# A graph-attention layer on one core: where the last eight blocks of x are loaded and added

## The chip, the core and the metric

The kernel runs on one core of a Trainium2 chip. The core has a matrix engine (TensorE, PE in the profile), a vector engine (VectorE, DVE), an activation engine (ScalarE, ACT), a general engine (GpSimd, POOL) and a sequencer that mostly issues transfers (SyncE, SP). Each takes its instructions in order; they wait for one another by semaphores. The metric is the device time of one execution in microseconds, as the median of several runs.

## What is computed

```python
ht = (h @ W).reshape(N, 4, 512)            # 4 heads
e = leaky_relu(src[:, :, None] + dst[:, None, :], 0.01) + adj[None]
att = softmax(e, axis=-1)
x_out = layernorm(x + mean_over_heads(att @ ht))
```

Here x is 4096 x 512 and adj is 4096 x 4096, both float32; W is 512 x 2048. The entries of adj go up to 1e9 and lie far apart, so that a row's softmax is 1 at the row's largest entry and 0 elsewhere as long as the largest entry leads the second by more than a bound on the other terms. Then a row of the output is layernorm(x[i] + x[j] @ mean of the heads' W), with j the column of the largest entry of row i of adj.

## The kernel before, in words

The rows are dealt out to 128 partitions in 32 blocks (NB = 32): partition p has rows 32 p to 32 p + 31, and block ib is row 32 p + ib of every partition. A block of adj is 2 MB, a block of x, of gathered rows or of the output 256 KB. `LATE` is 28, `Q` is 4.

`leading_rows` does the work above for all rows, and counts the rows in which the largest entry does not lead by enough. `general` (a full softmax for such rows) runs only if there are any; with these inputs it does not run.

The main loop runs over t = 0 to 31, and each pass works on several blocks:

- SyncE issues the load of adj block t + 5 (`load_adj`, six buffers), and in some passes a load of x into `hold` (`load_x`). All loads go through one queue in the order of issue, so a block of adj that stands behind a block of x lands after it. A block of adj comes in 1, 2 or 4 pieces (`pieces`).
- VectorE takes the maximum of each 64 entries of block t (`segment_maxima`, line 155; in two groups, with `find_column` of block t - 2 between them) and finds the segment with the row's maximum (`find_segment`).
- GpSimd fetches that segment's 64 entries (`lead`, line 168). Two passes later VectorE finds the column in it (`find_column`, line 190) and, for the later test, the two largest of it (`find_inner`, line 184). GpSimd then gathers the row of x that belongs to the column (`y`, line 178).
- TensorE transposes y of block t - 3 (`turn`, line 205), ScalarE copies the result out (line 207), TensorE puts x of the block into PSUM by a product with the identity (`residual`, line 211) and adds y times the mean W in four products (`products`, line 218; each is two matmul records in the trace).
- ScalarE sums block t - 4 and its squares (`stats`, lines 230 and 232) and the squares of x (`row_norm`, line 225), GpSimd makes the reciprocal deviation of two blocks (`rstd`, lines 235 to 237), and ScalarE normalises blocks t - 6 and t - 5 (`finish`, line 241).

After the loop comes the drain, written out by hand. For the last block `find_column_in_row` scans the whole row of adj (line 198), which needs no fetched segment. The last four blocks are normalised by `finish_last` on VectorE: add x (line 247), mean and variance (250, 252), a square root on ScalarE (254), reciprocal (255), scale (256). `bound`, `test`, `count` and `report` make the count of rows that don't lead; `bound` needs the row norms of all of x, `test` all of `inner`. SyncE issues the stores of the output (`store`, line 259) behind all loads: six of 1 MB for blocks 0 to 23, one of 256 KB for each later block; ScalarE issues block 31's.

The order around the change is thus set by three things: SyncE's queue, the order of the instructions on each engine as the code writes them, and the buffers. Before the change, `x_at` puts x of blocks 24 to 27 between the adj loads (x of 24 is ahead of adj 27, and so on), and x of 28 to 31 comes as one load of 1 MB behind all of adj.

Of the kernel before, what the change touches and what calls it, by code (L numbers as in the profile page):

```python
# [9 lines left out]
F32 = mybir.dt.float32  # L10
# [9 lines left out]
P = 128  # L20
C = 512
E = 64
# [43 lines left out]
def leading_rows(ctx, tc, x, adj, W, a, out, ident, v, n_bad, any_bad):  # L66
# [4 lines left out]

    nc = tc.nc
    N, D = x.shape
    H = a.shape[0]
    KB, NB, S = D // P, N // P, N // E
    AHEAD = 5
    Q = 4
    PIECES = 4  # L80
    LATE = NB - Q

    once = ctx.enter_context(tc.tile_pool(name="once", bufs=1))
    adj_pool = ctx.enter_context(tc.tile_pool(name="adj_pool", bufs=AHEAD + 1))
# [15 lines left out]
    adj_t = {}  # L100

    def pieces(ib):
        return PIECES if ib in (0, LATE, NB - 1) else 2 if ib > LATE else 1

    def load_adj(ib):
        if 0 <= ib < NB:
# [5 lines left out]
    def load_x(lo, n):  # L112
        nc.sync.dma_start(hold[:, ds(lo, n), :], x_rows[:, ds(lo, n), :])
# [46 lines left out]
    def find_segment(ib):  # L160
        seg = seg_of.pop(ib)
        nc.vector.max(out=top[:, ib, :], in_=seg)
        at = small.tile([P, 8], U32, name="at")
        nc.vector.max_index(at, top[:, ib, :], seg)  # L164
        row = small.tile([P, 1], U32, name="row")
        nc.gpsimd.tensor_tensor(row, at[:, 0:1], first[:, ib : ib + 1], op=OP.add)  # L166
        lead = small.tile([P, E], F32, name="lead")
        nc.gpsimd.indirect_dma_start(  # L168
            out=lead, out_offset=None, in_=adj_segs,
            in_offset=bass.IndirectOffsetOnAxis(ap=row[:, :1], axis=0),  # L170
        )
        start = at_of[ib] = small.tile([P, 1], U32, name="start")
        nc.gpsimd.tensor_tensor(start, at[:, 0:1], width, op=OP.mult)  # L173
        lead_of[ib] = lead
# [8 lines left out]
    def find_inner(ib):  # L183
        nc.vector.max(out=inner[:, ib, :], in_=lead_of[ib])

    def find_column(ib):
        if ib != NB - 2:
            find_inner(ib)
        within = small.tile([P, 8], U32, name="within")
        nc.vector.max_index(within, top[:, ib, :], lead_of[ib])  # L190
        col = small.tile([P, 1], U32, name="col")
        nc.gpsimd.tensor_tensor(col, at_of.pop(ib), within[:, 0:1], op=OP.add)  # L192
        gather_rows(ib, col)
# [7 lines left out]
    def turn(ib):  # L201
        y = y_t.pop(ib)
        tp = psum.tile([P, KB, P], F32, name="tp", bufs=2)
        for kb in range(KB):
            nc.tensor.transpose(tp[:, kb, :], y[:, ts(kb, P)], ident)  # L205
        yt = yt_of[ib] = rows.tile([P, KB, P], F32, name="yt")
        nc.scalar.copy(yt, tp)  # L207
# [5 lines left out]
    def products(ib, lo=0, hi=KB):  # L213
        start = ib not in o_ps
        if start:
            o_ps[ib] = psum.tile([P, D], F32, name="o")
        for kb in range(lo, hi):
            nc.tensor.matmul(  # L218
                o_ps[ib], yt_of[ib][:, kb, :], w_sum[:, kb, :],
                start=(start and kb == 0), stop=(kb == KB - 1),  # L220
            )

    def row_norm(ib):
        sq = rows.tile([P, D], F32, name="sq")
        nc.scalar.activation(sq, hold[:, ib, :], AF.Square, accum_out=xx[:, ib : ib + 1])  # L225

    def stats(ib):
        o, i = o_ps[ib], slice(ib, ib + 1)
# [5 lines left out]
    def rstd(i):  # L234
        nc.gpsimd.tensor_scalar(sd[:, i], sd[:, i], 1.0 / D, EPS, op0=OP.mult, op1=OP.add)  # L235
        nc.gpsimd.tensor_tensor(sd[:, i], sd[:, i], power[:, : i.stop - i.start], op=OP.pow)  # L236
        nc.gpsimd.tensor_mul(nm[:, i], nm[:, i], sd[:, i])  # L237

    def finish(ib):
        i = slice(ib, ib + 1)  # L240
        nc.scalar.activation(hold[:, ib, :], o_ps.pop(ib), AF.Identity, bias=nm[:, i], scale=sd[:, i])  # L241

    def finish_last(ib, residual):

        o = o_ps.pop(ib)
        if residual:
            nc.vector.tensor_add(hold[:, ib, :], o, hold[:, ib, :])
            o = hold[:, ib, :]
        st = small.tile([P, nc.vector.BN_STATS_DIM], F32, name="st", bufs=2)
        nc.vector.bn_stats(st, o)  # L250
        mv = small.tile([P, nc.vector.BN_AGGR_DIM], F32, name="mv", bufs=2)
        nc.vector.bn_aggr(mv, st)
        r = small.tile([P, 1], F32, name="r", bufs=2)
        nc.scalar.activation(r, mv[:, 1:2], AF.Sqrt, bias=eps)
        nc.vector.reciprocal(r, r)
        nc.vector.tensor_scalar(hold[:, ib, :], o, mv[:, 0:1], r, op0=OP.subtract, op1=OP.mult)

    def store(queue, lo, n):
        queue.dma_start(out_rows[:, ds(lo, n), :], hold[:, ds(lo, n), :])
# [49 lines left out]
    def bound(part):  # L309

        if part == 0:
            xm = once.tile([P, 1], F32, name="xm")
            nc.vector.tensor_reduce(xm, xx, axis=AX.X, op=OP.max)
            px = of_bound[0] = psum.tile([1, P], F32, name="px", bufs=1)
            nc.tensor.transpose(px, xm, ident)
        elif part == 1:
            nc.vector.tensor_reduce(xg, of_bound[0], axis=AX.X, op=OP.max)
            nc.scalar.activation(xg, xg, AF.Sqrt)
            pb = of_bound[1] = psum.tile([P, 1], F32, name="px", bufs=1)
            nc.tensor.matmul(pb, ones[0:1, :], xg, start=True, stop=True)  # L320
        else:
            nc.vector.tensor_mul(lead_by, of_bound[1], vn)
            nc.vector.tensor_scalar(lead_by, lead_by, 1.05, 110.0, op0=OP.mult, op1=OP.add)
# [18 lines left out]
    def report(pg):  # L342
        nc.vector.tensor_scalar(n_bad, pg, -1.0, float(P), op0=OP.mult, op1=OP.add)
        total = once.tile([1, 1], F32, name="total")
        nc.vector.tensor_reduce(total, pg, axis=AX.X, op=OP.add)
        nc.vector.tensor_scalar(any_bad, total, -1.0, float(N), op0=OP.mult, op1=OP.add)

    x_at = {lo - 1: (lo, Q) for lo in range(Q, LATE - Q, Q)}
    x_at.update({ib - 2: (ib, 1) for ib in range(LATE - Q, LATE)})
    vectors = [(kb, h) for kb in range(KB) for h in range(H)]  # L350
    vectors_at = {t: 2 if t < 3 else 1 for t in range(1, 15)}
    COLUMN, PROJECT, STATS, FINISH = 2, 3, 4, 6
# [1 line left out]
    for t in range(NB):  # L354
        if t in x_at:
            load_x(*x_at[t])
        load_adj(t + AHEAD)
        middle = 1 if t == NB - 1 else 2
        segment_maxima(t, 0, middle)
        if t >= COLUMN:  # L360
            find_column(t - COLUMN)
        segment_maxima(t, middle, PIECES)
        pair = t >= FINISH and t % 2 == 0
        if pair:
            rstd(slice(t - FINISH, t - FINISH + 2))
        find_segment(t)
        if t < 2:
            mean_of_heads(t)
        elif t == 2:
            mean_of_heads(2)  # L370
            mean_of_heads(3)
        if t == 0:
            turn_a()
        turned = [(*vectors[0], turn_w(*vectors.pop(0))) for _ in range(vectors_at.get(t, 0))]
        if t == 16:
            head_norms()
        ib = t - PROJECT
        if ib >= 0:
            turn(ib)
            if ib < LATE:  # L380
                residual(ib)
        for some in turned:
            head_vector(*some)
        if ib >= 0:
            products(ib)
        if t >= STATS:
            stats(t - STATS)
            row_norm(t - STATS)
        if pair:
            finish(t - FINISH)  # L390
            finish(t - FINISH + 1)

    load_x(LATE, NB - LATE)
    for lo in range(0, NB - 2 * Q, Q):
        store(nc.sync, lo, Q)
    for ib in range(NB - 2 * Q, NB - FINISH):
        store(nc.sync, ib, 1)
    find_column(NB - 2)
    rstd(slice(NB - FINISH, NB - FINISH + 2))
    find_column_in_row(NB - 1)  # L400
    for ib in range(LATE, NB):
        row_norm(ib)
    turn(NB - 3)
    products(NB - 3, 0, KB - 1)
    finish(NB - FINISH)
    finish(NB - FINISH + 1)
    bound(0)
    finish_last(NB - 4, True)
    find_inner(NB - 2)
    find_inner(NB - 1)  # L410
    turn(NB - 2)
    products(NB - 3, KB - 1, KB)
    residual(NB - 1)
    products(NB - 2, 0, 1)
    bound(1)
    products(NB - 2, 1, KB - 1)
    finish_last(NB - 3, True)
    turn(NB - 1)
    bound(2)
    test()  # L420
    products(NB - 2, KB - 1, KB)
    for ib in range(NB - FINISH, NB - 2):
        store(nc.sync, ib, 1)
    products(NB - 1, 0, KB - 1)
    pg = count()
    products(NB - 1, KB - 1, KB)
    finish_last(NB - 2, True)
    store(nc.sync, NB - 2, 1)
    report(pg)
    finish_last(NB - 1, False)  # L430
    store(nc.scalar, NB - 1, 1)

# [233 lines left out]
```

## Time and profile before

| what | us |
|---|---|
| median of 7 runs | 247.32 (246.19 to 248.61) |
| the profiled execution's own time | 246.12 |
| its span in the profile | 244.1 |
| PE busy | 197.0 (81%) |
| DVE busy | 186.1 (76%), of which line 155: 146.1 |
| ACT busy | 109.8 (45%) |
| POOL busy | 97.4 (40%) |
| bytes moved by DMA | 97.76 MB, mean 401 GB/s |

The profile is of one execution. All times in it count from the start of its span. A line of the timeline has the start, the duration, the engine, the line of the kernel, the operation, output<-input with shapes, and in brackets how long the engine was idle before it and what ended that wait. A line of the chain of work has start, duration and what ran. A line of the table by stage has the stage, its length, the busy time of PE, PE's weight loads, DVE, ACT and POOL with the number of instructions, the granted clock of TensorE, the busy share of the DMA engines and what they moved in GB/s.

### The profile page before, as it was taken

What the parts mean: (1) busy time and instruction counts of PE and PEld (TensorE: products, weight loads), DVE (VectorE), ACT (ScalarE), POOL (GpSimd) and SP (SyncE); (2) the same over time, 40 slices, a digit from 0 to 9 for tenths busy, and PEclk for the clock granted to TensorE, in tenths of its full rate; (3) what the DMA queues carried; (4) which work ended last, traced back from release to release, by engine and by line L of the source; (5) the groups of instructions that cost most, each with busy time, mean ns of one, the idle gap of its engine ahead of it and who ended that gap; (6) DMA issues with size and microseconds to landing.
All of it is one profiled execution on the core that took longest, in us unless ns stands there. A gap on an engine that the chain in (4) does not pass through costs nothing.

```text
span 244.1 us, 2481 instructions
## 1 busy us (share of the span) xinstructions
PE 197.0 (81%) x677; PEld 99.3 (41%) x678; DVE 186.1 (76%) x300; ACT 109.8 (45%) x266; POOL 97.4 (40%) x213
## 2 busy tenths in 40 slices
PE   0269749999999899999959977798768989877970
PEld 0125326556565556655324423343323433332520
DVE  2645685399689886999589969985998998978561
ACT  2012002145757574757635653556344846476110
POOL 1202422226525643645254636453546464653000
PEclk9999989999999999999988999999999999999995
DMA  7999999999999999999999999999999999999971
GB/s 258 434 430 412 418 430 419 413 424 424 408 419 417 405 431 417 415 408 433 412 421 414 424 411 418 414 416 420 423 416 389 407 407 406 404 426 424 419 281 55
DMA packets 13988, 97.76 MB, mean 401 GB/s; under 512 B 2184, under 2 KB 2184, under 8 KB 7824
## 3 DMA queue, kind: packets, MB, share of 16 engines
q1 hardware_dynamic: 10224, 87.82, 87.2%
q0 software_dynamic: 3584, 9.44, 9.9%
q10 hardware_dynamic: 160, 0.28, 0.3%
q8 instruction: 7, 0.11, 0.2%
q14 instruction: 13, 0.11, 0.1%
HBM read 89.15 MB, written 8.39 MB: 400 GB/s over the span
## 4 chain that ended last, share of the span: by engine, by line
issue 37%; POOL 34%; DMA 18%; PE 4%; DVE 3%; POOLq 1%; SPq 1%; ACT 0%
DMA adj_t<-in_adj_dram 15%; POOL lead L168 11%; POOL y L178 11%; POOL sd L236 4%; PE o L218 3%; DMA y<-in_x_dram,col 3%; POOL start L173 2%; POOL col L192 2%; POOL row L166 2%; DVE seg L155 2%; POOL sd L235 1%; POOL nm L237 1%; SPq L110 1%; POOLq L178 0%; PE tp L205 0%
## 5 line engine op out<-in xcount | busy, mean ns | idle before, releaser
L155 DVE TENSOR_REDUCE seg<-adj_t 128x32 f32<-128x2048 f32 (+1 forms) x70 | 146.1, 2093 | 40.5 <-DMA adj_t<-in_adj_dram 40.0
L218 PE MATMUL o<-w_sum,yt 128*128 128x512 f32 x256 | 119.8, 609 | 1.5 <-ACT yt L207 1.5
L218 PEld LDWEIGHTS o<-w_sum,yt 128*128 128x128 f32 x256 | 46.5, 192 | 58.4 <-issue 45.4
L207 ACT COPY yt<-tp 128x512 f32<-128x512 f32 x32 | 18.8, 587 | 49.0 <-PE tp L205 42.7
L178 POOL DMA_INDIRECT y<-in_x_dram,col x32 | 30.8, 964 | 17.8 <-POOL col L192 15.7
L168 POOL DMA_INDIRECT lead<-in_adj_dram,row x32 | 32.2, 1008 | 13.9 <-POOL row L166 13.9
L205 PE MATMUL tp<-ident,y 128*128 128x128 f32 x128 | 19.7, 277 | 16.6 <-DMA y<-in_x_dram,col 16.5
L264 PE MATMUL o<-hold,ident 128*128 128x512 f32 x32 | 17.9, 713 | 17.9 <-DMA hold<-in_L_gnn_W_dram 17.9
L211 PE MATMUL o<-hold,ident 128*128 128x512 f32 x58 | 29.9, 598 | 0.0
L192 POOL TENSOR_TENSOR col<-start,within 128x1 uint32<-128x1 uint32 x31 | 5.9, 189 | 52.5 <-DVE within L190 52.5
L205 PEld LDWEIGHTS tp<-ident,y 128*128 128x128 f32 x128 | 14.1, 141 | 31.1 <-issue 27.6
L282 ACT COPY wt<-tp 128x512 f32<-128x512 f32 x16 | 9.2, 587 | 31.6 <-PE tp L280 30.0
L166 POOL TENSOR_TENSOR row<-at,first 128x1 uint32<-128x1 uint32 x32 | 6.1, 189 | 37.8 <-DVE at L164 37.8
L241 ACT ACTIVATE hold<-o,nm,sd 128x512 f32<-128x512 f32 x28 | 20.1, 770 | 0.0
L225 ACT ACTIVATE sq<-hold 128x512 f32<-128x512 f32 x32 | 19.8, 618 | 0.0
L232 ACT ACTIVATE sq<-o,nm 128x512 f32<-128x512 f32 x28 | 19.3, 688 | 0.9
L288 PEld LDWEIGHTS pv<-at_d,wt 128*128 128x128 f32 x128 | 16.3, 191 | 6.8 <-ACT wt L282 3.5
L264 PEld LDWEIGHTS o<-hold,ident 128*128 128x128 f32 x32 | 7.0, 229 | 26.2 <-POOL row L166 10.4
L265 ACT ACTIVATE w_sum<-o 128x512 f32<-128x512 f32 x4 | 2.4, 598 | 33.5 <-PE o L264 33.5
L230 ACT ACTIVATE sq<-o 128x512 f32<-128x512 f32 x28 | 17.0, 606 | 0.0
L288 PE MATMUL pv<-at_d,wt 128*128 128x2 f32 x128 | 15.3, 244 | 0.6 <-ACT wt L282 0.6
L280 PEld LDWEIGHTS tp<-ident,hold 128*128 128x128 f32 x64 | 7.9, 142 | 6.9 <-issue 6.9
(73 smaller groups left out, 115.7 us busy)
## 6 DMA issues: line engine op xcount, KB each, us to landing
adj_t<-in_adj_dram SPq DMA_DIRECT2D x27, 2048.0 KB, 33.5
hold<-in_x_dram SPq DMA_DIRECT2D x7, 1024.0 KB, 34.0
adj_t<-in_adj_dram SPq DMA_DIRECT2D x12, 512.0 KB, 10.3
out_dram<-hold SPq DMA_DIRECT2D x6, 1024.0 KB, 21.8
hold<-in_L_gnn_W_dram SPq DMA_DIRECT2D x4, 1024.0 KB
adj_t<-in_adj_dram SPq DMA_DIRECT2D x4, 1024.0 KB
out_dram<-hold SPq DMA_DIRECT2D x7, 256.0 KB, 3.0
hold<-in_x_dram SPq DMA_DIRECT2D x4, 256.0 KB, 13.1
```

Source lines behind the costliest of these rows:

```text
L155: nc.vector.tensor_reduce(seg_of[ib][:, ts(k, S // n)], adj_t[ib][:, ts(k, N // n)].rearrange("p (s e) -> p s e", e=E), axis=AX.X, op=OP.max,)
L168: nc.gpsimd.indirect_dma_start(out=lead, out_offset=None, in_=adj_segs, in_offset=bass.IndirectOffsetOnAxis(ap=row[:, :1], axis=0),)
L178: nc.gpsimd.indirect_dma_start(out=y, out_offset=None, in_=x, in_offset=bass.IndirectOffsetOnAxis(ap=col[:, :1], axis=0),)
L205: nc.tensor.transpose(tp[:, kb, :], y[:, ts(kb, P)], ident)
L207: nc.scalar.copy(yt, tp)
L211: nc.tensor.matmul(o_ps[ib], ident, hold[:, ib, :], start=True, stop=False)
L218: nc.tensor.matmul(o_ps[ib], yt_of[ib][:, kb, :], w_sum[:, kb, :], start=(start and kb == 0), stop=(kb == KB - 1),)
L225: nc.scalar.activation(sq, hold[:, ib, :], AF.Square, accum_out=xx[:, ib : ib + 1])
L232: nc.scalar.activation(sq, o, AF.Square, bias=nm[:, i], accum_out=sd[:, i])
L241: nc.scalar.activation(hold[:, ib, :], o_ps.pop(ib), AF.Identity, bias=nm[:, i], scale=sd[:, i])
L264: nc.tensor.matmul(o, ident, hold[:, w_at + kb * H + h, :], start=(h == 0), stop=(h == H - 1))
L288: nc.tensor.matmul(pv[:, kb, h : 2 * H : H], wt[:, k, :], at_d[:, k, h : 2 * H : H], start=(k == 0), stop=(k == KB - 1),)
```

## The change

`BEHIND` is 24. x of blocks 24 to 31 is loaded behind all of adj, in eight loads of 256 KB; blocks 24 to 27 have no `residual` in TensorE's sum. In the loop, ScalarE copies the bare products of these four blocks into a buffer of the adj pool (`put_by`) instead of doing `stats`, `row_norm` and `finish` on them. In the drain VectorE adds x to them (`add_x`, both operands in SBUF), ScalarE does their `stats`, GpSimd their `rstd`, and ScalarE normalises them (`finish`). All eight `row_norm`s of blocks 24 to 31 and all eight `find_inner`s stand in the drain. adj blocks 28 to 31 come in four pieces each, and in passes 29 to 31 `find_column` stands behind the first piece instead of behind the first half. All stores have 256 KB, and the last seven are issued by SyncE behind `report`.

```diff
-        return PIECES if ib in (0, LATE, NB - 1) else 2 if ib > LATE else 1
+        return PIECES if ib == 0 or ib >= LATE else 1
...
-        lead = small.tile([P, E], F32, name="lead")
+        lead = small.tile([P, E], F32, name="lead", bufs=2 * Q + 1)
...
-        if ib != NB - 2:
+        if ib < BEHIND:
             find_inner(ib)
...
+    def put_by(ib):
+        if ib == BEHIND:
+            o_ps["by"] = adj_pool.tile([P, N // D, D], F32, name="adj_t")
+        nc.scalar.copy(o_ps["by"][:, ib - BEHIND, :], o_ps.pop(ib))
+
+    def add_x(ib):
+        nc.vector.tensor_add(hold[:, ib, :], hold[:, ib, :], o_ps["by"][:, ib - BEHIND, :])
+        o_ps[ib] = hold[:, ib, :]
...
-    x_at = {lo - 1: (lo, Q) for lo in range(Q, LATE - Q, Q)}
-    x_at.update({ib - 2: (ib, 1) for ib in range(LATE - Q, LATE)})
+    x_at = {lo - 1: (lo, Q) for lo in range(Q, BEHIND, Q)}
...
-        middle = 1 if t == NB - 1 else 2
+        middle = 1 if t > LATE else 2
...
-        pair = t >= FINISH and t % 2 == 0
+        pair = FINISH <= t < BEHIND + FINISH and t % 2 == 0
...
-            if ib < LATE:
+            if ib < BEHIND:
                 residual(ib)
...
-        if t >= STATS:
+        if t >= BEHIND + STATS:
+            put_by(t - STATS)
+        elif t >= STATS:
             stats(t - STATS)
             row_norm(t - STATS)
...
-    load_x(LATE, NB - LATE)
-    for lo in range(0, NB - 2 * Q, Q):
-        store(nc.sync, lo, Q)
-    for ib in range(NB - 2 * Q, NB - FINISH):
+    for ib in range(BEHIND, NB):
+        load_x(ib, 1)
+    for ib in range(BEHIND):
         store(nc.sync, ib, 1)
     find_column(NB - 2)
-    rstd(slice(NB - FINISH, NB - FINISH + 2))
     find_column_in_row(NB - 1)
-    for ib in range(LATE, NB):
+    for ib in range(BEHIND, NB - 2):
         row_norm(ib)
     turn(NB - 3)
+    for ib in range(NB - 2, NB):
+        row_norm(ib)
     products(NB - 3, 0, KB - 1)
-    finish(NB - FINISH)
-    finish(NB - FINISH + 1)
+    finish_last(NB - 4, True)
     bound(0)
-    finish_last(NB - 4, True)
-    find_inner(NB - 2)
-    find_inner(NB - 1)
     turn(NB - 2)
+    add_x(BEHIND)
+    add_x(BEHIND + 1)
     products(NB - 3, KB - 1, KB)
     residual(NB - 1)
     products(NB - 2, 0, 1)
     bound(1)
     products(NB - 2, 1, KB - 1)
+    add_x(BEHIND + 2)
+    add_x(BEHIND + 3)
+    stats(BEHIND)
+    stats(BEHIND + 1)
+    rstd(slice(BEHIND, BEHIND + 2))
     finish_last(NB - 3, True)
+    stats(BEHIND + 2)
     turn(NB - 1)
+    finish(BEHIND)
+    finish(BEHIND + 1)
+    stats(BEHIND + 3)
+    rstd(slice(BEHIND + 2, LATE))
+    for ib in range(BEHIND, NB):
+        find_inner(ib)
     bound(2)
     test()
     products(NB - 2, KB - 1, KB)
-    for ib in range(NB - FINISH, NB - 2):
-        store(nc.sync, ib, 1)
     products(NB - 1, 0, KB - 1)
     pg = count()
     products(NB - 1, KB - 1, KB)
     finish_last(NB - 2, True)
-    store(nc.sync, NB - 2, 1)
+    finish(BEHIND + 2)
+    finish(BEHIND + 3)
     report(pg)
+    for ib in (NB - 4, NB - 3, BEHIND, BEHIND + 1, NB - 2, BEHIND + 2, BEHIND + 3):
+        store(nc.sync, ib, 1)
     finish_last(NB - 1, False)
     store(nc.scalar, NB - 1, 1)
```

More of the change, by code (lines that the diff above doesn't have):

```diff
@@ L81, in leading_rows @@
     LATE = NB - Q
+    BEHIND = LATE - Q
     once = ctx.enter_context(tc.tile_pool(name="once", bufs=1))
```

## The prediction

> **What bounds the kernel now.** I read the page's slices first, then the waits, then the end of the chain of work, then VectorE's timeline over the last blocks, then the table by stage of the DMA rate. The page's span and DMA rows:
>
> ```profile
> span 244.1 us, 2481 instructions
> DMA  7999999999999999999999999999999999999971
> GB/s 258 434 430 412 418 430 419 413 424 424 408 419 417 405 431 417 415 408 433 412 421 414 424 411 418 414 416 420 423 416 389 407 407 406 404 426 424 419 281 55
> ```
>
> The DMA engines are full from 6 us to about 235 us. Only the last 9 us are not transfer. So the order of transfers decides when the last work can begin, and the sum of bytes sets a floor. The chain's end shows what follows the last gathers:
>
> ```profile
> 218.63 7.10 DMA y<-in_x_dram,col
> ...
> 225.86 0.63 PE tp L205 x4
> ...
> 231.72 3.57 PE o L218 x8
> ...
> 238.01 0.81 DVE hold L256
> ```
>
> Block 30's gather lands at 225.72; TensorE then works almost without a gap to 236.5, VectorE normalises block 31 to 238.82, the last store is issued at 238.86. What made that gather start at 218.63 stands in VectorE's timeline:
>
> ```profile
> 187.90 2.29 DVE L155 TENSOR_REDUCE seg<-adj_t 128x32 f32<-128x2048 f32 x1 [0.86 <-DMA adj_t<-in_adj_dram]
> ...
> 190.11 0.22 DVE L184 MAX8 inner<-lead 128x8 f32<-128x64 f32 x1
> 190.24 0.07 DVE L190 MATCH_VALUE_LOAD within<-top,lead 128x8 f32 x1
> ...
> 205.17 2.29 DVE L155 TENSOR_REDUCE seg<-adj_t 128x32 f32<-128x2048 f32 x1 [0.97 <-DMA adj_t<-in_adj_dram]
> ...
> 216.04 0.22 DVE L164 FIND_INDEX8 at<-top,seg 128x8 uint32<-128x64 f32 x1
> 217.48 0.09 DVE L190 MATCH_VALUE_LOAD within<-top,lead 128x8 f32 x1 [1.22 <-DMA lead<-in_adj_dram,row]
> ...
> 217.82 4.42 DVE L198 FIND_INDEX8 col<-top,adj_t 128x8 uint32<-128x4096 f32 x1
> ```
>
> VectorE waits for adj before blocks 27 (0.86) and 30 (0.97); otherwise it is back to back from 187.90 to 216.26, 5.4 to 5.5 us a block. So two limits lie close together: transfers (a 2 MB adj block, a 256 KB x block and a 256 KB gather) and VectorE.
>
> **The change, part by part.**
>
> *x of 24 to 27 leaves the adj stream.* Four x blocks are 1.05 MB; at the 404 to 406 GB/s of that stretch (rows below) 2.6 us. Adj 27 lands 0.65 sooner (one x block was ahead of it), adj 30 and 31 2.6 sooner. VectorE can't take all of it: block 27 starts 0.65 sooner (187.25), block 30's wait of 0.97 goes, and next it is bound by itself.
>
> *find_inner of 24 to 31 moves to the drain.* MAX8 takes the pipe 0.13 (190.11 to 190.24); five blocks on this path save 0.65. Blocks 29 and 30 are reduced in 4 pieces, not 2: 2.33 a half instead of 2.28, about 0.2 back. Sum: block 31's segment search ends 0.65 + 0.97 + 0.65 - 0.1 = 2.2 us sooner, at 214.05 instead of 216.26.
>
> *The column search one piece sooner (29, 30).* The search for block t-2 then stands 5.35 + 1.15 = 6.5 behind that block's own segment search. The lead row it reads took 0.87 to be issued and 5.6 to 6.1 to land: 6.5 to 7.0. At 6.5 nothing waits; at 7.0 VectorE stalls 0.5 in up to three blocks. Beside 4 KB rows the leads landed in the shorter of these times; I take 0.2 in all, bounds 0 and 1.5.
>
> *Last columns.* Lead 30 is issued at about 209.4 and lands by 215.0; block 31's scan of 4.42 runs 215.3 to 219.8 (before 217.82 to 222.24). The gather of y30 keeps its distance of 2.37 from the segment search of 31 (GpSimd does row, lead and start in between): 216.5, and lands 6.1 to 7.1 later (6.1 is a gather beside 4 KB rows in this trace, 7.1 beside 8 KB), 222.6 to 223.6 against 225.72.
>
> *ScalarE in the loop.* A put_by copy (L207's 0.59) replaces stats and row_norm (0.61 + 0.20 + 0.69 + 0.19 + 0.62 + 0.19, less overlap: 2.0). Four residual matmul pairs of 0.86 go too. Neither engine ends a wait there: nothing gained. The eight row_norms (0.61 each, 4.9) stand partly before the copy of yt29. x29 should land near 216, the six norms end near 217 and y29's transposes near 217.8: covered by 0.8, and if x is later the copy is late by as much.
>
> *The drain on VectorE,* from the end of the scan to the last tensor_scalar. Before: 222.24 to 238.82, 16.6, of which 1.98 + 1.27 + 0.60 were waits for TensorE. Added: 4 add_x and 6 more MAX8. add_x reads two SBUF tiles, which no row shows; the nearest is L247 (one PSUM operand) at 0.69. Back to back I take 0.60 to 0.70: 2.4 to 2.8. MAX8: 6 x 0.14 = 0.8. Together 3.2 to 3.6, into waits of 3.85. The waits don't all survive: TensorE's chain also starts sooner. Following the three orders op by op, scan end 219.7, y30 222.6: finish_last(28) to 222.3, two adds and xg to 223.9, two adds to 225.1, finish_last(29) to 228.1 with 0.5 waiting for ScalarE (two stats of 1.41 are queued ahead of its sqrt), MAX8s to 229.3, test to 230.7, finish_last(30) to 233.4, report to 233.8, finish_last(31) to 236.3. ScalarE's last sqrt sits behind finish(26) and finish(27), which wait for stats(27) and a 1.27 us GpSimd chain: 0.2 to 0.3, included. TensorE ends at 233.3 and is not late. With y30 at 223.6 the end is 237.0. So the last store is issued at 236.3 to 237.1, against 238.86.
>
> A rule of the Trainium skill speaks against this part. GPSIMD Engine Reference, section Specifications, says that GpSimd shares its SBUF interface with VectorE and is held up by VectorE instructions with two SBUF inputs. The adds run 222.4 to 225.1, while GpSimd writes y31's descriptors. In the trace y31, issued at 223.00 beside adds with one SBUF operand, was there without a wait when TensorE turned it at 231.12. In the changed kernel it is issued at about 220.5 and lands, at y30's 6.5 or so, at 227. By the rule it could be 2.4 later, 229.4, and TensorE, which wants it at 228.1, would lose 1.3. I take nothing and keep 1.3 as the bound.
>
> *Transfers at the end.* Stores of blocks 0 to 23 become 24 of 256 KB (2 KB rows) instead of six of 1 MB; x 24 to 31 eight loads of 256 KB; blocks 29 and 30 finer. By stage (DMA share and GB/s are the last two columns):
>
> ```profile
> 206.00:212.00 6.00, 4.81 (x15) 1.97 (x14) 5.82 (x11) 2.38 (x7) 3.00 (x8) 1.00 1.02 399
> 212.00:230.00 18.00, 15.00 (x45) 6.81 (x44) 13.73 (x27) 10.82 (x28) 6.56 (x13) 1.00 1.02 424
> 232.00:234.00 2.00, 2.00 (x6) 0.83 (x5) 1.35 (x2) 0.40 (x1) 0.00 (x0) 1.00 1.01 393
> 234.00:236.00 2.00, 2.00 (x8) 0.61 (x6) 1.35 (x7) 0.29 (x1) 0.00 (x0) 1.00 0.70 269
> ```
>
> 206 to 212 is block 31 in quarters, 212 to 230 mostly 1 MB stores, 232 to 234 256 KB stores alone. From 186 to the end the rows add up to 20.9 MB. At 398 GB/s (the finer rows) that takes 52.5 us: to 238.5, where the last bytes before left at about 240.8. The rule of DMA: Bandwidth & Descriptors, section Bandwidth, is to batch DMAs to 1 MiB for 75% of peak, and it puts 1 MB at 341 GB/s and 64 KB at 138. By it, 256 KB stores at some 250 GB/s (an estimate between these figures) would need 33 us for 8.1 MB instead of 20, and the kernel would be 10 us slower. The row decides: several stores are in flight at once, and 256 KB ones ran at 393. Their issues cost SyncE 0.33 each against 0.65 of transfer: hidden.
>
> Compute frees the last store at 236.3 to 237.1; its 1.9 us after that (238.86 to 240.8 before) would end at 238.2 to 239.0; transfers allow 238.5. I take 239.0, which is 1.8 sooner. Span 242.3; that run's own 246.12 becomes 244.3; it stood 1.2 below the median, and the same 1.8 off the median 247.32 gives 245.5.
>
> **Rivals.** (1) *The drain eats it.* VectorE has no slack left after the scan, so each unforeseen wait there (leads 1.0, y31 1.3, ScalarE's order) shows in full. For it: two in-order engines tie at the end. Against: the path's every other duration is in a row. A loss of 1 us more leaves 0.8: 246.5, within 0.5%. (2) *The change does not bring columns sooner*, because VectorE, not adj, is the limit: only the 0.65 and part of 0.97 remain, also about 246.5. Against it: the row at 205.17 waits for DMA. (3) *Slower: the cut stores.* If x and stores of 2 KB rows run below the rest, transfers set the end. It decides once the mean from 186 on falls below 20.9 MB / 54.8 us = 381 GB/s. At 340 for these 10.2 MB and 398 for the other 10.7: 26.9 + 30.0, so 242.9, 2.1 later than before: 249.4. For it: 393 is the lowest full row, and only eight transfers can be outstanding, now 2 MB instead of 8. Against: that row had at most six outstanding.
>
> **How the numbers follow.** About 0.5% (1.2 us) is what a measurement of this kernel can tell from no change. Forecast 0.64 (244.3 to 246.0), rivals 1 and 2 together 0.22 (246 to 247.7), rival 3 0.14 (247.7 to 250). Low end: transfers at 411 GB/s as before end at 236.9 and compute allows 2.6 to 3: 244.3. High end 247.7: leaves out rival 3 and the edge below. Faster 0.64, same 0.22, slower 0.14.
>
> **What would show it.** Right: no DMA wait before block 30's reduce; scan of block 31 starting near 215.3; VectorE almost gapless after it; last store issued near 236.5; 390 to 405 GB/s from 216 to 234. Wrong: the wait for leads in three blocks; a late copy of yt29 or yt31 behind ScalarE's norms or stats; DMA rows under 380 with the last stores queued behind others.

## The result, and the profile after

The changed kernel takes 245.38 us (median of 23 runs, 244.79 to 246.72), the kernel before 246.85 (60 runs, 245.57 to 249.32). The ratio is 0.994 with an interval of 0.9925 to 0.9955: 1.5 us sooner, where 1.8 were forecast. In the experiments each ratio is against runs of the kernel before from the same set (their medians run from 246.51 to 247.16), so it is not exactly the quotient of two medians shown here.

The profiled execution of the changed kernel took 245.75 us. Its span, transfers and rates:

```profile
span 243.7 us, 2537 instructions
...
DMA  6999999999999999999999999999999999999993
GB/s 247 409 426 419 426 422 414 429 415 409 423 416 418 407 427 416 424 406 426 411 419 418 425 420 416 409 420 412 419 422 392 403 403 399 389 393 397 403 376 118
```

The engines that move data are now full to the last slice but one; before, the last two slices read 7 and 1. VectorE's timeline of this execution, at the places that were shown of before:

```profile
182.16 2.29 DVE L157 TENSOR_REDUCE seg<-adj_t 128x32 f32<-128x2048 f32 x1 [0.34 <-DMA adj_t<-in_adj_dram]
...
214.43 0.22 DVE L166 FIND_INDEX8 at<-top,seg 128x8 uint32<-128x64 f32 x1
216.27 0.09 DVE L192 MATCH_VALUE_LOAD within<-top,lead 128x8 f32 x1 [1.63 <-DMA lead<-in_adj_dram,row]
...
216.61 4.42 DVE L200 FIND_INDEX8 col<-top,adj_t 128x8 uint32<-128x4096 f32 x1
```

The wait for adj ahead of block 30 (0.97) is gone, and block 31's segment search comes at 214.43 instead of 216.04. Then VectorE waits 1.63 for the fetched segment of block 30 (1.22 before), so its scan starts only 1.2 sooner.

The chain that ended last, in the same execution (start, duration, what ran):

```profile
215.37 5.40 PE o L220 x8
...
225.30 0.59 ACT yt L209
...
235.37 0.87 ACT hold L253 x2
236.24 0.55 issue
236.79 0.29 ACT r L266
...
237.30 0.81 DVE hold L268
```

Two things are new. The eight product records of block 28 took 5.40; in a second profiled execution of this kernel (below) they took 3.71. And from 225.30 on the chain runs through ScalarE, not through TensorE. The table by stage shows both (the last three columns are the granted clock of TensorE, the share of the transfer engines and GB/s):

```profile
212.00:230.00 18.00, 15.49 (x43) 6.87 (x42) 14.44 (x27) 11.35 (x34) 4.99 (x9) 0.91 1.05 396
...
232.00:234.00 2.00, 2.00 (x7) 0.62 (x5) 1.57 (x4) 1.97 (x6) 0.00 (x0) 1.00 1.05 402
234.00:236.00 2.00, 1.23 (x5) 0.33 (x4) 1.67 (x7) 0.82 (x3) 1.08 (x3) 1.00 0.99 380
```

The granted clock was 0.91 over 212 to 230 (1.00 before) and 0.76 over 214 to 221, and ScalarE is busy nearly all of 232 to 234 (1.97 of 2.00). Since a clock like that may belong to one execution, the same kernel was profiled again, as one of the experiments.

### The profile page after: what moved, and what is told of

It is laid out like the page before. It is cut to its first block, busy times and chain, and to the rows that moved or that the text cites. A ratio compares the mean times of both kernels' runs of the same rounds, so it can differ in the third digit from the quotient of the medians.

```text
span 243.7 us, 2537 instructions
## 1 busy us (share of the span) xinstructions
PE 199.6 (82%) x669; PEld 101.1 (41%) x670; DVE 188.2 (77%) x308; ACT 111.9 (46%) x270; POOL 97.3 (40%) x213
## 4 chain that ended last, share of the span: by engine, by line
issue 34%; POOL 32%; DMA 19%; ACT 4%; PE 4%; DVE 3%; POOLq 1%; SPq 1%; ACTq 0%
DMA adj_t<-in_adj_dram 15%; POOL lead L170 10%; POOL y L180 10%; POOL sd L248 4%; PE o L220 3%; DMA y<-in_x_dram,col 3%; POOL start L175 2%; POOL col L194 2%; POOL row L168 2%; DVE seg L157 2%; ACT sq L244 1%; POOL sd L247 1%; ACT sq L242 1%; POOL nm L249 1%; ACT yt L209 1%
## 5 line engine op out<-in xcount | busy, mean ns | idle before, releaser
L220 PE MATMUL o<-w_sum,yt 128*128 128x512 f32 x256 | 121.3, 615 | 4.2 <-ACT yt L209 4.2
L220 PEld LDWEIGHTS o<-w_sum,yt 128*128 128x128 f32 x256 | 47.4, 195 | 61.1 <-issue 47.3
L207 PEld LDWEIGHTS tp<-ident,y 128*128 128x128 f32 x128 | 14.9, 144 | 25.8 <-issue 25.1
L276 PEld LDWEIGHTS o<-hold,ident 128*128 128x128 f32 x32 | 8.0, 264 | 25.8 <-POOL row L168 11.3
L253 ACT ACTIVATE hold<-o,nm,sd 128x512 f32<-128x512 f32 x24 | 17.2, 771 | 0.0
L244 ACT ACTIVATE sq<-o,nm 128x512 f32<-128x512 f32 x24 | 16.5, 687 | 0.8
L242 ACT ACTIVATE sq<-o 128x512 f32<-128x512 f32 x24 | 14.6, 607 | 0.0
```

The costliest lines, as they stand in the source:

```text
L220: nc.tensor.matmul(o_ps[ib], yt_of[ib][:, kb, :], w_sum[:, kb, :], start=(start and kb == 0), stop=(kb == KB - 1),)
L244: nc.scalar.activation(sq, o, AF.Square, bias=nm[:, i], accum_out=sd[:, i])
L276: nc.tensor.matmul(o, ident, hold[:, w_at + kb * H + h, :], start=(h == 0), stop=(h == H - 1))
```

## The experiments

**The changed kernel once more** (no edit).

> The changed kernel itself, on the same chip as the three beside it: 0.9925 to 0.9955. Theory of the stall (2 KB rows slow the gather of the lead of block 30): its stall before block 31's scan is 1.2 to 1.8 us again, and the scan starts 1.0 to 1.4 us sooner than in the kernel before. Rival (the stall belonged to the one execution, as did TensorE's clock of 0.76): the stall is under 0.7.

245.37 us, ratio 0.9949 (0.9924 to 0.9974). Its profiled execution took 244.77, with a span of 242.8. VectorE's timeline:

```profile
181.43 2.29 DVE L157 TENSOR_REDUCE seg<-adj_t 128x32 f32<-128x2048 f32 x1 [0.35 <-DMA adj_t<-in_adj_dram]
...
213.70 0.22 DVE L166 FIND_INDEX8 at<-top,seg 128x8 uint32<-128x64 f32 x1
215.60 0.09 DVE L192 MATCH_VALUE_LOAD within<-top,lead 128x8 f32 x1 [1.68 <-DMA lead<-in_adj_dram,row]
...
215.93 4.42 DVE L200 FIND_INDEX8 col<-top,adj_t 128x8 uint32<-128x4096 f32 x1
```

The first row stood at 182.16 in the other execution, so that one lagged by 0.7 already there, and keeps that distance to the scan. The stall of 1.7 for the lead is there again. The scan starts 1.9 sooner than before the change, somewhat more than the 1.0 to 1.4 that was expected. The table by stage of this execution:

```profile
212.00:230.00 18.00, 14.60 (x47) 6.87 (x47) 14.95 (x37) 12.84 (x37) 4.56 (x9) 1.00 1.05 398
...
234.00:236.00 2.00, 0.00 (x0) 0.00 (x0) 1.01 (x4) 1.69 (x3) 0.00 (x0) 1.00 1.04 399
236.00:238.00 2.00, 0.00 (x0) 0.00 (x0) 0.74 (x1) 0.00 (x0) 0.00 (x0) 0.81 0.91 344
238.00:239.00 1.00, 0.00 (x0) 0.00 (x0) 0.00 (x0) 0.00 (x0) 0.00 (x0) 0.50 0.74 270
```

The clock is 1.00 here, and the last store is issued at 236.77 (238.14 in the other execution, 238.86 before the change). But the transfer engines are full to 236, busy for 0.91 of the time to 238, and SyncE's last bytes leave at 239.2. So compute and transfers end nearly together here. (In the first execution compute came last: the engines ran at 0.89 from 236 to 238, and the last store was issued 1.4 later.) The next experiments take the two apart.

**Does x, moved behind adj, bring the gain?** x of 24 to 27 back between the adj loads, everything else as changed:

```diff
+    x_at.update({ib - 2: (ib, 1) for ib in range(BEHIND, LATE)})
-    for ib in range(BEHIND, NB):
+    for ib in range(LATE, NB):
         load_x(ib, 1)
```

> Undoes one part of the change: x of blocks 24 to 27 is loaded between the adj blocks again, all else is as in the changed kernel. My theory (the gain comes from adj landing up to 2.6 us sooner, and VectorE takes about 2 of it): the DMA wait before block 30's reduce is back, the scan of block 31 starts 1 to 2 us later than in the changed kernel, and the time goes to 0.998 to 1.004 of the kernel before. Rival (the gain comes from finding the columns one piece sooner and from the lighter loop on ScalarE and TensorE): the time stays at 0.994.

246.54 us, ratio 0.9963 (0.993 to 0.9996). Its timeline of VectorE:

```profile
207.05 2.49 DVE L157 TENSOR_REDUCE seg<-adj_t 128x16 f32<-128x1024 f32 x2 [0.72 <-DMA adj_t<-in_adj_dram]
...
215.95 0.22 DVE L166 FIND_INDEX8 at<-top,seg 128x8 uint32<-128x64 f32 x1
216.40 0.09 DVE L192 MATCH_VALUE_LOAD within<-top,lead 128x8 f32 x1 [0.23 <-DMA lead<-in_adj_dram,row]
```

The waits for adj are back, and block 31's search comes 2.25 later than in the second execution above, which this one matches up to block 26 (181.44 against 181.43). The stall for the lead shrinks from 1.68 to 0.23 at the same time, so the scan (216.73) is only 0.8 later. In the same set of runs the two variants below that keep x behind adj take 245.30 and 245.62. The move is thus worth about 1 us of the 1.5: nine of the twelve runs here (245.67 to 247.09) lie above the slowest of the twelve of x in pairs (244.66 to 245.95), though the intervals of the two ratios overlap. The ratio is lower than the 0.998 to 1.004 that was expected, so part of the gain doesn't hang on the move; which other part of the change brings it, no run here takes apart.

**Are finer last blocks enough?** The kernel before, with only the four pieces for blocks 28 to 31 and the earlier column search:

```diff
-        return PIECES if ib in (0, LATE, NB - 1) else 2 if ib > LATE else 1
+        return PIECES if ib == 0 or ib >= LATE else 1
...
-        middle = 1 if t == NB - 1 else 2
+        middle = 1 if t > LATE else 2
```

> The kernel before with one part of the change alone: adj blocks 28 to 31 in four pieces and the column search behind the first piece in passes 29 to 31. My theory: y of 27 to 29 is gathered 1 us sooner but the scan of block 31 starts at the same time, so 0.999 to 1.001. Rival (late columns carry the gain): 0.996 or below.

247.22 us, ratio 1.0007 (0.9973 to 1.004), scan at 217.87 (217.82 before). These two parts alone bring nothing sooner.

**Do the 2 KB rows of x make the stall?** x of 24 to 31 in four loads of two blocks (4 KB rows):

```diff
-    for ib in range(BEHIND, NB):
-        load_x(ib, 1)
+    for ib in range(BEHIND, NB, 2):
+        load_x(ib, 2)
```

> The changed kernel with x of 24 to 31 in four loads of two blocks (4 KB rows) instead of eight of one (2 KB rows). In the changed kernel's profile the gathers beside 2 KB rows moved their bytes in 2.5 to 3.1 us, beside 4 KB rows in 1.5, and the fetched segment of block 30 came 1.6 us after VectorE was ready. If the row size is the cause: VectorE's wait before block 30's column falls from 1.6 to 0.8 or less, and the kernel gains 0.3 to 1.0 us on the changed one (0.990 to 0.993 of before). If the number of outstanding bytes or something else is the cause: the wait stays at 1.6 and the time at 0.994.

245.30 us, ratio 0.9921 (0.9887 to 0.9955). VectorE's timeline:

```profile
211.05 0.09 DVE L192 MATCH_VALUE_LOAD within<-top,lead 128x8 f32 x1 [0.51 <-DMA lead<-in_adj_dram,row]
...
215.60 0.09 DVE L192 MATCH_VALUE_LOAD within<-top,lead 128x8 f32 x1 [0.22 <-DMA lead<-in_adj_dram,row]
```

The stall for lead 30 falls to 0.22, but 0.51 of it moves to lead 29, and the time stays. So far it looks as if the 2 KB rows made the stall. The other runs' profiles don't bear that out. Eight profiled executions do the same work up to the scan (the two of the changed kernel, and the variants below and after this one that edit only the drain or the stores). In four of them the last bytes of lead 30 came 5.47 to 5.53 after its issue, and the stall was 1.58 to 1.76; in three they came after 4.67 to 4.74, and it was 0.85 to 0.93; in one lead 29 was the late one. Beside 4 KB rows both times are seen too: the two later variants with x in pairs have 4.55 and 4.67 (stalls of 0.80 and 0.90), while here lead 29 took 5.43, and in the kernel before lead 29 took 5.45. So in kernels that are alike up to this point there are two landing times, 0.8 apart (in the kernel before, lead 30 took 5.03, between the two), and a floor of 0.8 to 0.9 under the stall; that 2 KB rows make the later one likelier is not shown. The late lead does not come alone. In the four executions with a late lead 30, the gather y28, still under way when that lead was issued, was late too: its last bytes came 6.9 to 7.2 after its issue, against 5.5 to 5.6 in the three with an early lead; in the one with a late lead 29 it was y27 (7.0, against 5.7). Something holds up GpSimd's gathers once, for about 1 us, and what it is stays open.

**Is it ScalarE's order at the end?** Roots of 26 and 27 apart, and `finish(26)` ahead of block 30's square root:

```diff
     stats(BEHIND + 2)
+    rstd(slice(BEHIND + 2, BEHIND + 3))
     turn(NB - 1)
...
     stats(BEHIND + 3)
-    rstd(slice(BEHIND + 2, LATE))
+    rstd(slice(BEHIND + 3, LATE))
+    finish(BEHIND + 2)
...
-    finish(BEHIND + 2)
     finish(BEHIND + 3)
```

> The changed kernel with GpSimd's reciprocal deviation of blocks 26 and 27 made one by one, and block 26 normalised ahead of block 30's square root. If ScalarE's queue holds the end (its last square root waited 0.6 us behind two normalisations): VectorE's last wait falls from 0.9 to 0.4 us and the kernel gains 0.3 to 0.6 us on the changed one (0.992). If the last stores' transfers hold the end: the wait falls and the time stays at 0.994.

245.62 us, ratio 0.9944 (0.9913 to 0.9975). VectorE's wait ahead of the last reciprocal fell from 0.92 (first execution) to 0.36, the round trip to ScalarE and back; the one ahead of block 30's grew from 0.58 to 1.27:

```profile
235.44 0.17 DVE L267 RECIPROCAL r<-r 128x1 f32<-128x1 f32 x1 [1.27 <-ACT r L266]
...
237.73 0.16 DVE L267 RECIPROCAL r<-r 128x1 f32<-128x1 f32 x1 [0.36 <-ACT r L266]
```

The wait was moved, not removed.

**Do the cut stores hold up the end?** Stores of 0 to 23 in twelve pairs, and, in a second kernel, in six of 1 MB (the same lines with `Q` in place of 2):

```diff
-    for ib in range(BEHIND):
-        store(nc.sync, ib, 1)
+    for ib in range(0, BEHIND, 2):
+        store(nc.sync, ib, 2)
```

> The changed kernel with the stores of blocks 0 to 23 as twelve of two blocks (4 KB rows) instead of twenty-four of one. Theory (the end is set by compute: the last store is issued when ScalarE and VectorE have finished, and transfers have bytes to spare then): the rate from 221 to 234 us rises from 399 to 402 towards 411 to 425, the last store's issue moves by less than 0.4 us, ratio to the kernel before 0.992 to 0.996, that is no change against 0.994. Rival (the cut stores hold up the end, as transfers or through slower gathers of y30 and y31): the end comes 0.7 to 1 us sooner, 0.990 to 0.991.

> The changed kernel with the stores of blocks 0 to 23 as six of 1 MB again (8 KB rows, as before the change). Theory: as with pairs, 0.992 to 0.997; the rate rises to some 420, but the gathers of y30 and y31 queue behind larger transfers (2.0 us of bytes against 1.45 beside 4 KB rows), so it isn't better than pairs. Rival (cut stores cost): 0.988 to 0.990.

245.43 us, 0.9938 (0.9916 to 0.9961), and 245.73 us, 0.9956 (0.9928 to 0.9985). With pairs, 221 to 228 ran at 420 GB/s instead of 402, but the last store was issued at 237.00 against 236.77, and the time stayed. So bigger stores alone give nothing that shows.

**Several at once.** x and stores in pairs, with the roots apart:

> The changed kernel with x of 24 to 31 in four loads of two blocks, stores of 0 to 23 in pairs, and the reciprocal roots of 26 and 27 apart with finish(26) ahead of the root of block 30. Theory: the stall for the lead of block 30 (1.6 us) falls to 0.5 and ScalarE's wait ahead of the last reciprocal (0.9) falls to 0.4, and both show because they stand on one chain: 1.2 to 1.6 us sooner than the changed kernel, 0.988 to 0.990. Rival (whatever is taken from one wait goes to another wait behind it, as with the split alone): 0.992 to 0.995.

245.17 us, 0.9946 (0.992 to 0.9973). The expected 0.988 to 0.990 didn't come. Its profiled execution had a clock of 0.76 in 221 to 228, so what its chain shows is no guide.

**Two limits at once?** Three kernels that leave work out, each in its own way. The first does without the statistics of 26 and 27, the second without the stores of 0 to 7, the third without both:

```diff
-    def finish(ib):
-        i = slice(ib, ib + 1)
+    def finish(ib, of=None):
+        of = ib if of is None else of
+        i = slice(of, of + 1)
...
-    stats(BEHIND + 2)
...
-    stats(BEHIND + 3)
-    rstd(slice(BEHIND + 2, LATE))
...
-    finish(BEHIND + 2)
-    finish(BEHIND + 3)
+    finish(BEHIND + 2, BEHIND)
+    finish(BEHIND + 3, BEHIND + 1)
```

```diff
-    for ib in range(BEHIND):
+    for ib in range(2 * Q, BEHIND):
         store(nc.sync, ib, 1)
```

> The changed kernel without the statistics of blocks 26 and 27: they are scaled with the mean and deviation of 24 and 25, so ScalarE loses two pairs of passes (2.9 us) and GpSimd one chain (1.3 us) in the drain; the outputs of 26 and 27 are not normalised by their own numbers. Theory (two limits tie at the end: ScalarE's queue, which frees the last store, and the transfers, which fill the 16 engines until 238): the store is issued up to 1 us sooner, but the transfers then hold it, 0 to 0.4 us sooner than the changed kernel, 0.993 to 0.995. Rival (ScalarE's queue alone sets the end): 0.7 to 1 us sooner, 0.990 to 0.992.

> The changed kernel without the stores of blocks 0 to 7: 2.1 MB less, some 5 us of transfer after 220; those rows of the output are not written. Theory (tie): the transfers end well before the last store, which ScalarE and VectorE issue when they did, 0.2 to 0.6 us sooner, 0.992 to 0.9945. Rival (transfers alone set the end, ScalarE's waits are idle anyway): 1.5 us sooner or more, 0.988 or less.

> Both of the two: without the statistics of 26 and 27 and without the stores of 0 to 7. Theory (tie): now it shows, 1.0 to 1.8 us sooner than the changed kernel, 0.987 to 0.990, more than the two single gains together. Rival (one limit alone): no more than the better of the two.

| kernel | us | ratio to before |
|---|---|---|
| changed | 245.37 | 0.9949 (0.9924 to 0.9974) |
| less for ScalarE | 245.10 | 0.9941 (0.9917 to 0.9964) |
| fewer stores | 244.73 | 0.9927 (0.9897 to 0.9956) |
| both | 243.41 | 0.9884 (0.985 to 0.9918) |

The changed kernel was run on another chip than the other three; the kernel before had the same median in both sets, 246.51. The single gains are 0.3 and 0.6 us, and neither is clear of the noise. Both at once give 2.0 (1.6 by the ratios), clear of the changed kernel by the intervals, and five of its six runs (243.15 to 244.45) lie below the fastest of the seven with fewer stores (244.33 to 245.57). That the joint gain exceeds the sum of the two, as it must where two limits tie, is likely but not beyond what six and seven runs can scatter. So the profiles have to carry the argument. The last store's issue in the changed kernel (second execution), with less for ScalarE, with fewer stores, and with both:

```profile
236.77 0.39 ACTq L271 DMA_DIRECT2D out_dram<-hold  x1
236.22 0.39 ACTq L272 DMA_DIRECT2D out_dram<-hold  x1
236.93 0.39 ACTq L271 DMA_DIRECT2D out_dram<-hold  x1
235.63 0.39 ACTq L272 DMA_DIRECT2D out_dram<-hold  x1
```

In the profile of the kernel with less for ScalarE, by stage:

```profile
234.00:236.00 2.00, 0.00 (x0) 0.00 (x0) 1.57 (x4) 0.44 (x2) 0.00 (x0) 1.00 1.04 397
236.00:238.00 2.00, 0.00 (x0) 0.00 (x0) 0.19 (x1) 0.00 (x0) 0.00 (x0) 0.68 1.04 391
```

Compute is over at 236.2, 0.55 sooner than in the changed kernel from a scan that began at the same time (215.97 against 215.93). But the transfers still run full to 238, and the last store was complete only at 241.84 (240.49 in the changed kernel): the gain of compute did not reach the end. (This execution took 245.97, 0.9 over its kernel's median, so how late its transfers ended is in part its own.) In the profile of the kernel with fewer stores:

```profile
228.00:234.00 6.00, 6.00 (x18) 2.21 (x17) 5.23 (x26) 4.92 (x12) 1.95 (x6) 1.00 0.47 177
...
236.00:238.00 2.00, 0.00 (x0) 0.00 (x0) 0.86 (x2) 0.00 (x0) 0.00 (x0) 1.00 0.73 267
```

The transfers are half idle from 228 to 234, and the last store still goes out at 236.93, when ScalarE and VectorE allow it; it was complete at 239.97. With both left out, the store goes out at 235.63 and is complete at 238.75, 1.7 sooner than in the changed kernel. About half of its earlier issue is this execution's early lead (its scan began at 215.38, 0.55 sooner). By stage:

```profile
236.00:238.00 2.00, 0.00 (x0) 0.00 (x0) 0.00 (x0) 0.00 (x0) 0.00 (x0) 0.58 0.41 146
```

In these profiles, then, sooner compute alone waits for transfers, fewer transfers alone wait mostly for compute, and with both the end moves.

**A version with all the work.** x and stores in pairs, blocks 24 and 25 normalised by GpSimd instead of ScalarE:

```diff
+    def finish_pool(ib):
+        i = slice(ib, ib + 1)
+        nc.gpsimd.tensor_scalar(hold[:, ib, :], o_ps.pop(ib), sd[:, i], nm[:, i], op0=OP.mult, op1=OP.add)
...
-    finish(BEHIND)
-    finish(BEHIND + 1)
+    finish_pool(BEHIND)
+    finish_pool(BEHIND + 1)
```

> The whole computation: the changed kernel with x of 24 to 31 and the stores of 0 to 23 in pairs, and blocks 24 and 25 scaled by GpSimd (idle from 229 to 232.7) in place of ScalarE, whose queue loses 1.4 us. Theory (tie): both limits give a little, 0.4 to 0.8 us sooner than the changed kernel, 0.991 to 0.993. Rival (GpSimd takes more than 3 us for two blocks, so that the roots of 26 and 27, behind them in its queue, are late, or it slows VectorE): no gain or a loss, 0.995 to 0.999.

244.76 us, ratio 0.9925 (0.9897 to 0.9952): the lowest median of the kernels that do all the work, 0.6 under the changed one, with intervals that overlap, so a gain on the changed kernel is not shown. Its group of GpSimd instructions (count, busy time, mean ns, idle time before):

```profile
L253 POOL TENSOR_SCALAR hold<-hold,sd,nm 128x512 f32<-128x512 f32 x2 | 1.6, 804 | 0.1
```

Two blocks cost 1.6 on an engine that was idle there; the rival's 3 us is wrong.

## Why the prediction was right, point by point

The second execution of the changed kernel, with a clock of 1.00 from 212 to 234, is the one to hold the sum against.

- *Block 31's segment search ends at 214.05.* Right: 213.92. Block 30's wait for adj is gone, as forecast. (The sum took off 0.1 for the finer pieces, where the sentence ahead of it had 0.2.)
- *Lead stalls of 0.2 in all; lead 30 by 215.0, scan at 215.3.* The stall in the loop was rightly put near nothing. For lead 30 the forecast left 0.95 (214.05 to 215.0) by taking its sooner landing time. Three of the eight executions have that (the scan at 215.40 and 215.38 in two of them, with pairs of stores and with both parts left out); in the second execution it landed 0.8 later, the stall was 1.68, and the scan began at 215.93, 0.6 late.
- *y30 issued at 216.5, landed by 222.6 to 223.6.* Issued at 216.70, its bytes moved by 222.3. The distance of 2.37 from the segment search was not kept: it was 2.78, since the column waited for the late lead; where the lead was early (both parts left out) it was 2.36. It ended no wait: TensorE turned it at 223.41 behind `bound(0)`, which waits for VectorE.
- *ScalarE in the loop and the row norms cost nothing.* Right, but barely: the six norms ended at 218.65 and not near 217, and the copy of yt29 behind them began at 218.72, as soon as TensorE had transposed y29 (it began that at 218.08). The 0.8 of cover was under 0.1.
- *VectorE's drain 16.6.* Right: 16.4 (scan end 220.35 to 236.74). The adds took 0.68 each, 0.60 apart.
- *ScalarE's order: 0.5 ahead of block 29's root, 0.2 to 0.3 ahead of the last.* The sum held, its places did not. VectorE's waits for the root in the second execution:

```profile
227.85 0.16 DVE L267 RECIPROCAL r<-r 128x1 f32<-128x1 f32 x1 [0.63 <-ACT r L266]
...
232.85 0.16 DVE L267 RECIPROCAL r<-r 128x1 f32<-128x1 f32 x1 [0.48 <-ACT r L266]
...
235.73 0.16 DVE L267 RECIPROCAL r<-r 128x1 f32<-128x1 f32 x1 [0.92 <-ACT r L266]
```

  Each has 0.36 of round trip in it, which is what is left where ScalarE is free; above that they lose 0.27, 0.12 and 0.56, 0.95 in all against 0.7 to 0.8.
- *Last store at 236.3 to 237.1.* 236.77. In the first execution, 238.14: 0.7 of the difference is its later beginning; the other 0.65 came after block 28's products, 1.7 longer at the lower clock.
- *Transfers at 398 GB/s, done at 238.5.* The rate was right (398 from 212 to 230), the end 0.7 later: SyncE's queue was done at 239.2, for from 236 on only the last stores were left and the rate fell to 344, then 270. The last store, issued into full engines, was complete 3.7 after its issue (240.49), where before the change it took 2.6 (238.86 to 241.42). The forecast had let it take what it took before, 1.9 from its issue to its last bytes; here that was 3.1. That is the mis-sized term: the last bytes left at 239.9 and not at 239.0. The span is only 0.5 longer than forecast (242.8 and not 242.3), because what follows the last bytes took 2.9 instead of 3.3, which is luck.
- *Median 245.5.* That 245.38 is so close is luck in part as well: 245.5 was 1.8 off a median of seven runs, 247.32, and the median of sixty is 246.85. The gain itself is 1.5.
- *Rivals.* The slower one (2 KB rows under 381 GB/s) fell: from 206 to 234 the two executions ran at 382 to 409 GB/s in stretches of 4 us, 396 and 398 over 212 to 230. The rule to batch transfers to 1 MiB (the Trainium skill, DMA: Bandwidth & Descriptors, section Bandwidth), from which the prediction estimated a cost of 10 us, does not price these stores: with several outstanding they ran at these rates. Pairs ran at up to 420 GB/s and the time stayed. The rival that the columns don't come sooner fell with x put back. The rival that the drain eats it was right in part: in the second execution it took 0.6 on the lead and 0.2 on ScalarE.
- *GpSimd and adds with two SBUF inputs.* That GpSimd's SBUF interface is shared and such adds contend for it (the Trainium skill, GPSIMD Engine Reference, section Specifications) is not tested here: y31's descriptors were written from 221.11 to 222.06, and the adds began at 223.00.

What the prediction missed is the tie itself. It had both ends, 236.3 to 237.1 plus 1.9 for compute and 238.5 for transfers, and took the later. It did not say that from there a gain on one side alone is worth next to nothing, and most of the experiments fit that. ScalarE's load in the drain shows how full the second engine of the chain has become (by line, second execution of the changed kernel, 222 to 240):

```profile
L253 ACT ACTIVATE hold<-hold,nm,sd 128x512 f32<-128x512 f32 x4 | 3.0, 806 | 1.2 <-POOL nm L249 1.2
L244 ACT ACTIVATE sq<-hold,nm 128x512 f32<-128x512 f32 x4 | 2.9, 722 | 0.1
L242 ACT ACTIVATE sq<-hold 128x512 f32<-128x512 f32 x4 | 2.5, 614 | 0.0
```

Of these 8.4 us only 1.4, two normalisations, were in that stretch before the change, where ScalarE waited 7.3 for VectorE's variances (line 252).

The low clock has a pattern in the traces. Their clock records show it as stretches of 3.41 us, seldom two in a row, at half clock; 0.76 and 0.91 are means over longer windows with one such stretch in them. In the first execution it was 215.55 to 218.97. That stretch and the one ahead of it, then the stretch of the second execution that holds the same gap in TensorE's work (the wait for y28), cut as its own clock record divides the time:

```profile
212.15:215.56 3.41, 1.57 (x7) 0.61 (x6) 2.36 (x5) 0.83 (x2) 0.80 (x3) 1.00 1.05 380
215.56:218.97 3.41, 3.41 (x5) 1.35 (x5) 2.70 (x4) 3.41 (x12) 2.18 (x4) 0.50 1.05 401
...
209.90:213.31 3.41, 2.36 (x7) 0.85 (x6) 3.38 (x4) 0.00 (x0) 1.71 (x4) 1.00 1.05 387
```

TensorE was busy for 0.46 of the stretch ahead of the half clock, and for 0.69 where none followed. Cut in this way, the fourteen traces have, from 60 to 233 us, 25 stretches at full clock in which TensorE was busy for less than 0.42: half clock followed all of them. Of 10 with 0.42 to 0.49 it followed four, and of 631 with more, none. So like work can draw a low clock or not, by where a gap in TensorE's work falls in these stretches. Six of the fourteen executions have one after 205 us, among them those with x back, with the roots apart, with stores of 1 MB, and with x and stores in pairs.

What stays open: what holds up a gather, and with it a lead, in some executions and not in others.

## What to carry to other kernels

When a change shortens the work and spreads the transfers at once, work out both ends and compare them: where they tie, an edit to one side measures as next to nothing, and it takes leaving out some of both to see the end move. A stall that is seen in two profiles may still be one of two values (1.6 to 1.8, or 0.9): compare all executions that do the same work up to that point before giving it a cause. The same comparison shows whether a low clock belongs to one execution, and the busy share of TensorE just ahead of it may say why.

## What was not expected of the hardware

- Beside 2 KB rows a gather of 256 KB began sooner and moved its bytes longer: in the two executions of the changed kernel the last four had their first bytes 2.6 to 4.3 after the issue and took 2.1 to 3.1, beside adj in 4 KB rows (y27) 4.3 and 1.4. The last bytes came at nearly the same time, 5.5 to 5.7 after the issue (6.9 and 7.0 for y28). They came 6.0 to 6.6 after it beside stores with 4 KB rows (y30 and y31 in the three kernels that have them), and 6.2 to 6.3 beside 8 KB rows in the kernel before (7.2 once).
- The fetch of one segment a row (leads 29 and 30) landed at one of two times after its issue, 4.5 to 4.8 or 5.4 to 5.5, in kernels that did the same up to it.
- TensorE's clock was halved for 3.41 us after a stretch of that length in which it was busy for less than about 0.42 to 0.49, without having been idle for long: in the first execution its longest wait there was 1.1 us.
- GpSimd scaled and shifted a 128x512 block in 0.80 us, as fast as ScalarE's 0.81 for the same work.
